# A two-layer state-space and mixture kernel: scans moved from 128 channels to 4 states x 32 channels on the partitions

## The chip, the cores and the metric

One core of a Trainium2 chip runs the whole program. The metric is the device time of one execution in microseconds (us). The engines are named as in the profile: PE multiplies matrices, DVE and POOL work elementwise (DVE also scans), ACT evaluates functions, SP issues the transfers (DMA).

## The reference

The input is `x`, 2 batches of 256 channels and 4096 positions, all in float32. It goes through a normalization over groups of channels and a state-space layer (256 inner channels), then through two layer normalizations and a forward and a backward state-space layer (512 inner channels each), then through a mixture of eight small networks. Each adds to a running `t`. The state-space layer is what matters here:

```
xs, z = split(seq @ W_in)                  # din inner channels each
xc    = silu(causal_conv4(xs))
dbc   = xc @ W_x                           # 16 for dt, 16 B, 16 C
dt    = softplus(dbc[:16] @ W_dt + b_dt)   # per channel and position
h[d,s] = h[d,s] * exp(dt[d] * A[d,s]) + dt[d] * xc[d] * B[s]     # along the 4096 positions
y[d]   = sum over s of h[d,s] * C[s] + xc[d] * D[d]
out    = (y * silu(z)) @ W_out
```

There are 16 states `s`, and `h` is carried along all positions.

## The kernel before

**Work.** Six jobs run one after the other: the first layer for two batches (2 blocks of 128 channels), the forward layer for two batches and the backward layer for two batches (4 blocks). Each job goes over its 4096 positions in 8 chunks of 512: 48 steps in `steps`, 16 narrow ones (`nj` = 2) and 32 wide ones (`nj` = 4). The mixture stage follows at the end.

**Quads.** In a step the scans go in quads `(i, jp, n)`: one pair `jp` of blocks and one pair `n` of states, so four rows of 128 partitions x 512 positions. A narrow step has 8 quads, a wide one 16. A partition is a channel. Per quad:
- SP loads two tiles, two rows of B and two of C, each spread from DRAM over all 128 partitions (`load_bc`, 512 KB each; the tile is called `bc`).
- POOL forms `bq = xdt * B` (`emit_b`, L533), where `xdt = dt * xc` is formed once per pair of blocks (L531).
- ACT forms the decays `da = exp(dt * a)` into PSUM, two per half quad (`emit_decay`, L546).
- DVE scans four rows (`emit_scan`, L556).
- The product with C is done by DVE for the quads n = 1, 4, 6, 7 (`emit_times_c`, L567) and by POOL for n = 0, 2, 3, 5 (`POOL_C`; `emit_times_c_quad`, L581). For the latter ACT first copies the last column into the carried state (`emit_carry`, L576).
- PE adds the states up into `y` in PSUM (`emit_sum`, L591) with an identity as the weight. It goes by quadrants of 64 rows x 64 columns (`TILES`). `y` starts with the skip term `xc * D` (`emit_skip`, L601), and `y` has one buffer, for a pair of blocks.
- DVE multiplies `y` with the gate `sz` (`emit_gate`, L608); PE projects (L623), DVE adds the residual (L631).

In what follows bN and cN are POOL's product with B and with C of quad N of a step (b8 in a narrow step is quad 0 of the next one).

**Order.** Every engine works strictly in the order in which the code writes to it (`in_order` ties each instruction to the one before it on its engine). The loop goes over slots, two per quad (s = 0 and 1), and in a slot writes for SP, PE, ACT, POOL and DVE in turn. Besides the scans of step i, the slots hold the preparation of step i + 1 (`prepare`): each operation is put into a slot and an engine's list by `sl.put`. In a wide step the projections and convolutions of the four blocks stand in slots 4 to 11, `dbc` in 14, and `softplus(j)` in slot 16 + j on PE, 17 + j on ACT, 18 + j on DVE; in a narrow step these are 0 to 3, 6, and 8 + j, 9 + j, 10 + j. POOL's products stand in the slots that `POOL_AT` gives:

```python
POOL_C = {0: 2, 2: 4, 3: 5, 5: 7}
POOL_AT = {0: "b3", 1: "c0 b4 b5", 3: "c2 b6", 4: "c3 b7", 6: "c5 b8 b9", 7: "b10"}
```

so at n = 1 POOL forms c of quad 0, then b of quads 4 and 5, in the first slot of that quad. `bq` has six buffers. The other tiles that matter: `dt` three buffers of a pair of blocks, `xdt` two, PSUM `ps` (projections, convolutions, dt) two.

**Buffers.** A tile whose pool has n buffers waits, when it is written the (n+1)th time, for every reader of the tile that had the buffer, a transfer among them.

## Time and profile before

| | us |
|---|---|
| median of 3 runs (6547.55 to 6551.92) | 6547.71 |
| the profiled execution | 6547.15 |
| its span, first to last instruction | 6545.3 |
| first scan | 52.1 |
| one narrow step (steps 9 to 13) | 56.4 to 56.6 |
| last narrow step, with the weights of the first wide one | 86.8 |
| one wide forward step | 119.9 |
| one wide backward step | 116.6 |

The times of the steps are from the timeline: from the first scan of a step to that of the next. A line of the profile names the source line, the engine, the operation and `out<-in` by the names of the tiles; `xN` is how many. One matrix product in float32 leaves two records. "Idle before" is how long the engine had nothing to do just before an instruction, and the arrow names what ended that. A timeline line gives the start and the length in us; neighbouring instructions of one kind are merged. A line of stretches gives, for a window of time, busy us (and the number of instructions) of PE, PE's weight loads, DVE, ACT and POOL, then the granted clock, the busy share of the DMA engines and GB/s.

### The profile page before, as it was taken

The page shows a single profiled execution, that of the slowest core. Times are in us where ns is not written, and L with a number is a line of the kernel's source. Part 1 is how long each engine was busy: PE and PEld are TensorE (multiplying, and loading weights), DVE is VectorE, ACT ScalarE, POOL GpSimd, SP SyncE. Part 2 cuts the span into 40 slices and gives each one's busy share as a digit, 9 for nine tenths or more (in the row PEclk, how much of TensorE's full clock was granted, in tenths as well). Part 3 has the DMA queues.
Part 4 walks back from the last instruction along what each step waited for, and adds up shares of the span by engine and source line. Part 5 has one row for each costly group of instructions (what it writes and reads, how often), then busy time and mean ns, then how long its engine had stood idle before and what let it go on. Part 6 is the DMA issues. An engine that isn't in the chain of part 4 may idle for free.

```text
span 6545.3 us, 53913 instructions
## 1 busy us (share of the span) xinstructions
PE 5210.1 (80%) x18600; PEld 1864.2 (28%) x18600; DVE 4695.0 (72%) x4889; ACT 3286.2 (50%) x5057; POOL 4530.5 (69%) x1062
## 2 busy tenths in 40 slices
PE   6778777877777778777777777777669999999999
PEld 2222222222222222222222222222124444444444
DVE  7999998999999999998999999999921111111111
ACT  5666665565565555655555555565522222222222
POOL 7999988999999999999999999999910000000000
PEclk9888888988988888889888898888879999999989
DMA  5545454445445444444444444444410000000000
GB/s 181 184 172 184 176 177 152 155 166 170 161 158 174 156 164 161 164 162 164 152 169 155 156 161 156 163 162 159 162 64 11 2 13 13 13 0 13 13 7 7
DMA packets 254229, 806.98 MB, mean 123 GB/s; under 512 B 26362, under 2 KB 35330, under 8 KB 253954
## 3 DMA queue, kind: packets, MB, share of 16 engines
q1 hardware_dynamic: 253954, 803.53, 35.8%
q8 instruction: 146, 2.39, 0.1%
q14 instruction: 129, 1.06, 0.1%
HBM read 749.95 MB, written 53.48 MB: 123 GB/s over the span
## 4 chain that ended last, share of the span: by engine, by line
PE 41%; DVE 34%; ACT 11%; issue 9%; POOL 4%; DMA 1%; SPq 0%; DVEq 0%; POOLq 0%; ACTq 0%
DVE da L556 16%; PE hp L863 14%; DVE bq L556 9%; PE conv L383 7%; PE ym L897 7%; ACT da L546 4%; PE y L591 4%; DVE bq L567 4%; PE xs L348 3%; POOL bq L533 2%; PE o L623 2%; POOL bq L581 1%; PE wb L888 1%; DVE xc L397 1%; DMA bc<-bcd 1%
## 5 line engine op out<-in xcount | busy, mean ns | idle before, releaser
L533 POOL TENSOR_TENSOR bq<-xdt,bc 128x2048 f32<-128x2048 f32 x640 | 2882.5, 4527 | 6.3
L546 ACT ACTIVATE da<-dt,w_a 128x512 f32<-128x512 f32 x2560 | 1766.0, 690 | 1350.9 <-DVE h_state L570 1122.5
L591 PE MATMUL y<-bq,ident 64*64 64x512 f32 x10240 | 1396.4, 666 | 477.5 <-DVE bq L567 424.7
L581 POOL TENSOR_TENSOR bq<-bq,bc 128x2048 f32<-128x2048 f32 x320 | 1448.1, 4525 | 171.0 <-ACT h_state L576 171.0
L556 DVE TENSOR_TENSOR_SCAN da<-da,h_state,bq 128x512 f32<-128x512 f32 x1120 | 1437.4, 1283 | 86.9 <-issue 66.5
L556 DVE TENSOR_TENSOR_SCAN bq<-da,h_state,bq 128x512 f32<-128x512 f32 x1120 | 1363.1, 1266 | 3.9 <-ACT da L546 2.4
L867 ACT ACTIVATE h<-hp,of,sc 128x512 f32<-128x512 f32 x512 | 397.8, 777 | 1024.8 <-PE hp L863 1024.8
L567 DVE TENSOR_TENSOR bq<-da,bc 128x1024 f32<-128x1024 f32 x640 | 783.9, 1225 | 36.9 <-DMA bc<-bcd 9.1
L894 DVE TENSOR_TENSOR h<-h,wbs 128x1024 f32<-128x1024 f32 x128 | 156.9, 1226 | 874.7 <-ACT h L867 874.7
L591 PEld LDWEIGHTS y<-bq,ident 64*64 64x64 f32 x10240 | 359.4, 146 | 1480.2 <-DVE bq L567 695.7
L383 PE MATMUL conv<-xs,w_conv 128*128 128x512 f32 x1280 | 589.4, 603 | 43.1 <-ACT xs L373 24.5
L863 PE MATMUL hp<-n,W 128*128 128x512 f32 x1024 | 490.6, 634 | 0.0
L348 PE MATMUL z<-nx,w_in 128*128 128x512 f32 x640 | 358.0, 698 | 134.1 <-DVE sz L466 109.1
L863 PE MATMUL hp<-h,W 128*128 128x512 f32 x1024 | 449.9, 592 | 0.0
L897 PE MATMUL ym<-h,Wo 128*128 128x512 f32 x1024 | 449.9, 592 | 0.0
L430 PE MATMUL dt<-dbc,w_dt 128*128 128x512 f32 x320 | 238.8, 839 | 241.4 <-DVE dt L445 191.2
L383 PEld LDWEIGHTS conv<-xs,w_conv 128*128 128x128 f32 x1280 | 233.2, 190 | 392.7 <-issue 261.5
L623 PE MATMUL o<-sz,w_out 128*128 128x512 f32 x640 | 342.7, 681 | 1.5 <-DVE sz L608 1.4
L348 PE MATMUL xs<-nx,w_in 128*128 128x512 f32 x640 | 322.8, 629 | 22.8 <-DVE xr L631 19.6
L863 PEld LDWEIGHTS hp<-n,W 128*128 128x128 f32 x1024 | 201.1, 202 | 293.3 <-issue 293.3
L890 DVE COPY wbs<-wb 128x512 f32<-128x512 f32 x64 | 44.2, 691 | 320.6 <-PE wb L888 320.6
L601 PE MATMUL y<-xc,w_d 64*64 64x512 f32 x640 | 143.4, 984 | 155.4 <-DVE sz L608 155.4
(116 smaller groups left out, 4180.4 us busy)
## 6 DMA issues: line engine op xcount, KB each, us to landing
bc<-bcd SPq DMA_DIRECT2D x1280, 512.0 KB, 4.7
t_dram<-xr SPq DMA_DIRECT2D x48, 512.0 KB, 6.1
x<-t_dram SPq DMA_DIRECT2D x32, 512.0 KB, 5.7
xr<-t_dram SPq DMA_DIRECT2D x32, 512.0 KB, 6.5
x<-in_x SPq DMA_DIRECT2D x16, 512.0 KB, 5.4
xr<-in_x SPq DMA_DIRECT2D x16, 512.0 KB, 6.3
n_dram<-nx SPq DMA_DIRECT2D x16, 512.0 KB, 2.6
t_dram<-x SPq DMA_DIRECT2D x16, 512.0 KB, 3.4
```

Source lines behind the costliest of these rows:

```text
L348: nc.tensor.matmul(ps, job.w["in"][:, k, m * P : (m + 1) * P], rhs, start=(k == 0), stop=(k == KC - 1),)
L383: nc.tensor.matmul(v["ps"], w["conv"][:, j, k, :], job.xs[:, j, k : k + T], start=(k == 0), stop=(k == 3),)
L533: nc.gpsimd.tensor_tensor(bq[g], ck["xdt", jp].rearrange("p (o j) t -> p o j t", o=1).to_broadcast([P, 2, 2, T]), bt.pop(g).rearrange("p s ...
L546: nc.scalar.activation(da[g, s][:, j, :], cks[i]["dt", jp][:, j, :], AF.Exp, scale=steps[i][0].w["a"][:, 2 * jp + j, 2 * n + s : 2 * n + s ...
L556: nc.vector.tensor_tensor_scan(b if n in POOL_C else d[:, j, :], d[:, j, :], b, job.h[:, 2 * n + s, 2 * jp + j : 2 * jp + j + 1] if c else ...
L567: nc.vector.tensor_tensor(bq[g][:, s, :, :], d, ct[g][:, s : s + 1, :].to_broadcast([P, 2, T]), ALU.mult)
L581: nc.gpsimd.tensor_tensor(bq[g], bq[g], ct[g].rearrange("p s (o t) -> p s o t", o=1).to_broadcast([P, 2, 2, T]), ALU.mult,)
L591: nc.tensor.matmul(y[i, jp][out_, r, :], ident[rows, rows], bq[g][rows, s, j, :], start=False, stop=(n == QN - 1 and s == 1),)
L623: nc.tensor.matmul(v[m], job.w["out"][:, j, m * P : (m + 1) * P], ck["sz", j // 2][:, j % 2, :], start=(j == 0), stop=(j == job.nj - 1),)
L863: nc.tensor.matmul(ps, w[:, k, m * P : (m + 1) * P], x[:, k, :], start=(k == 0), stop=(k == KC - 1),)
L867: nc.scalar.activation(h[:, m, :], ps, AF.Relu, bias=of[:, l, e, m : m + 1], scale=sc[:, l, e, m : m + 1],)
L897: nc.tensor.matmul(y[:, b, m, :], we["Wo", e][:, k, m * P : (m + 1) * P], h2[b][:, k, :], start=False, stop=(e == E - 1 and k == KC - 1),)
```

## The change

A partition now holds one of 4 states and one of 32 channels. A quad is one block `j` and one group `sg` of 4 states; its four rows `q` are the four groups of 32 channels of the block. B and C tiles hold a group of 4 states, each state copied to 32 partitions (`load_states`, 256 KB), and serve all blocks of a step: 8 loads per step, 5 buffers each. In exchange `dt` and `xdt` must be spread, so that each of four groups of 32 partitions holds all 128 channels of a block as 4 rows of 32: after DVE's `dt` and POOL's `xdt` (now one per block, written in slot s + 2 of `softplus`), SP stores both to DRAM (slots s + 3 and s + 4), and `load_rep` reads each back in four transfers of 256 KB to 32 partitions. `load_later` gives each load the slot from which it may be issued, and `flush` issues those that are due and whose source has been written. The sum over the states becomes, per quad, four products of 128 rows x 32 columns with the weight `stack`, one for each row `q`, all after the quad's end. `y` holds one block and has two buffers; skip and gate go by block. `dt` and `xdt` have two buffers of one block each. W_out is loaded when its job starts, and the skip weights later. The host reorders the decay weights, and no longer reorders z and W_out.

```diff
-QN = NS // 2
-TILES = [(r, col, (col - r) % 2) for r, col in ((0, 0), (1, 1), (0, 1), (1, 0))]
+QN = 8
+SG = 4
+CG = P // SG
+POOL_AT_2 = {**POOL_AT, 6: "c5 b8", 7: "b9 b10"}
...
-        ps_y = st.enter_context(tc.tile_pool(name="ps_y", bufs=1, space=PSUM))
+        ps_y = st.enter_context(tc.tile_pool(name="ps_y", bufs=2, space=PSUM))
...
+        stack = const.tile([P, CG], F32, name="stack")
+        nc.vector.tensor_reduce(
+            stack, ident.rearrange("p (s c) -> p c s", s=SG), AX.X, ALU.add
+        )
...
                 def dve():
-                    dt = pair_tile(ck, "dt", j, tag, 3)
-                    nc.vector.scalar_tensor_tensor(dt, v["ps"], 0.0, v["th"], ALU.max, ALU.add)
-                    if j % 2:
-                        ck["dt_done", j // 2] = True
-                return pe, act, dve
+                    v["dt"] = wk.tile([P, T], F32, tag="dt", name=f"dt_{tag}_{j}", bufs=2)
+                    nc.vector.scalar_tensor_tensor(v["dt"], v["ps"], 0.0, v["th"], ALU.max, ALU.add)
+
+                def pool():
+                    v["xdt"] = wk.tile([P, T], F32, tag="xdt", name=f"xdt_{tag}_{j}", bufs=2)
+                    nc.gpsimd.tensor_tensor(v["xdt"], v["dt"], ck["xc", j], ALU.mult)
+
+                def store(key):
+                    d = ck["rep", key, j] = bcd.tile(
+                        [P, T], F32, tag=f"{key}{j}", name=f"{key}d_{tag}_{j}"
+                    )
+                    nc.sync.dma_start(d, v[key])
+
+                return pe, act, dve, pool, lambda: store("dt"), lambda: store("xdt")
...
             def put(s, fns):
-                for d, queue, fn in zip(range(3), ("pe", "act", "dve"), fns):
+                queues = ((0, "pe"), (1, "act"), (2, "dve"), (2, "pool"), (3, "sp"), (4, "sp"))
+                for (d, queue), fn in zip(queues, fns):
...
+        def load_states(i, h, sg):
+            t = bcp.tile([P, T], F32, tag=f"bc{h}", name=f"bc{h}_{tags[i]}_{sg}", bufs=5)
+            src = cks[i]["bc"][h, sg * SG : (sg + 1) * SG, :]
+            nc.sync.dma_start(
+                t, src.rearrange("s (o t) -> s o t", o=1).to_broadcast([SG, CG, T])
+            )
+            cks[i]["bc", h, sg] = t
+
+        def load_rep(i, key, j):
+            t = wk.tile([P, SG, T], F32, tag=f"r{key}", name=f"r{key}_{tags[i]}_{j}", bufs=2)
+            src = cks[i]["rep", key, j].rearrange("(q c) t -> c q t", q=SG)
+            for s in range(SG):
+                nc.sync.dma_start(t[s * CG : (s + 1) * CG], src)
+            cks[i]["r" + key, j] = t
+
+        def load_later(i, slot):
+            nj = steps[i][0].nj
+            for sg, (b, c) in enumerate(((-16, -16), (-13, -6), (-12, -1), (-9, 0))):
+                pending.append((slot + b, ("bc",), lambda sg=sg: load_states(i, 0, sg), i))
+                pending.append((slot + c, ("bc",), lambda sg=sg: load_states(i, 1, sg), i))
+            for j in range(nj):
+                for key, off in (("xdt", (-10, -12)[j % 2]), ("dt", -4)):
+                    pending.append(
+                        (slot + 8 * j + off, ("rep", key, j), lambda j=j, key=key: load_rep(i, key, j), i)
+                    )
+            pending.sort(key=lambda p: p[0])
+
+        def flush(slot):
+            for p in list(pending):
+                if p[0] <= slot and (p[1] if len(p[1]) > 1 else p[1][0]) in cks[p[3]]:
+                    pending.remove(p)
+                    p[2]()
...
+            nc.gpsimd.tensor_tensor(bq[g], ck["rxdt", j], over_groups(ck["bc", 0, sg]), ALU.mult)
...
+                    da[g, h][:, k, :], cks[i]["rdt", j][:, q, :], AF.Exp,
+                    scale=steps[i][0].w["a"][:, j, q * SG + sg : q * SG + sg + 1],
...
+        def emit_sum(g):
+            i, j, sg = at(g)
+            for q in range(SG):
+                nc.tensor.matmul(
+                    y[i, j][q * CG : (q + 1) * CG, :], stack, bq[g][:, q, :],
+                    start=False, stop=(sg == SG - 1),
                 )
...
-                    if first == 2 and last is not None:
-                        emit_gate(*last)
-                        last = None
-                    if first == 3:
-                        emit_skip(i, jp)
+                    if first in (2, 12) and done:
+                        emit_gate(*done.pop(0))
+                    if first in (1, 9):
+                        emit_skip(i, 2 * jp + first // 8)
...
-                    if s == 0:
-                        for what in POOL_AT.get(n, "").split():
+                    if h == 0:
+                        for what in (POOL_AT if wide else POOL_AT_2).get(n, "").split():
                             m = g - n + int(what[1:])
                             if what[0] == "c":
                                 emit_times_c_quad(m)
                             else:
-                                want(0, m + 3)
-                                flush()
                                 want_b(m)
-                    else:
-                        want(1, g + 2)
-                        flush()
                     sl.run(slot, "pool")
```

## The prediction

> **What bounds the kernel now.** I read the page first (engine shares), then the stretches of one step of each kind, then the timelines of POOL, DVE and PE inside them, then the waits.
>
> The page's first part gives busy time by engine, and its DMA issues give the median time to landing:
>
> ```profile
> PE 5210.1 (80%) x18600; PEld 1864.2 (28%) x18600; DVE 4695.0 (72%) x4889; ACT 3286.2 (50%) x5057; POOL 4530.5 (69%) x1062
> ...
> bc<-bcd SPq DMA_DIRECT2D x1280, 512.0 KB, 4.7
> n_dram<-nx SPq DMA_DIRECT2D x16, 512.0 KB, 2.6
> gx<-in_x SPq DMA_DIRECT2D x4, 1024.0 KB, 8.2
> ```
>
> The last quarter is the mixture stage, which the diff leaves alone. In the scans the stretches of one narrow step, one wide forward step and one wide backward step (start to start of the first scan) show who is full:
>
> ```profile
> core 0: us, PE busy (x) PEld busy (x) DVE busy (x) ACT busy (x) POOL busy (x), PEclk, DMA share, GB/s
> 579.30:635.90 56.60, 44.05 (x185) 13.48 (x184) 54.98 (x59) 36.74 (x57) 56.52 (x14) 0.91 0.54 179
> 2448.20:2568.20 120.00, 90.51 (x376) 28.61 (x376) 112.05 (x116) 70.55 (x112) 114.60 (x28) 0.88 0.48 163
> 3971.80:4088.40 116.60, 85.82 (x368) 27.65 (x368) 108.96 (x115) 66.24 (x105) 112.89 (x27) 0.88 0.46 160
> ```
>
> A narrow step is POOL from end to end (56.5 of 56.6). A wide step has 5.4 us (forward) or 3.7 us (backward) without POOL and some 8 us without DVE. DMA is half used, and the bytes that the change saves are on no path. What DVE waits for in the wide steps is seen in its waits between 2000 and 4000 us (17 steps):
>
> ```profile
> DVE xc L397 <- ACT thx L393: 73.8, 51, 2.0
> DVE da L556 <- issue: 36.3, 17, 2.4
> ```
>
> Both come from PE. Its timeline of one wide step (start, length, then the instructions merged):
>
> ```profile
> 2454.13 1.99 PE L601 MATMUL y<-xc,w_d 64*64 64x512 f32 x8 [3.91 <-DVE sz L608]
> ...
> 2472.65 3.60 PE L383 MATMUL conv<-xs,w_conv 128*128 128x512 f32 x8
> ...
> 2482.20 1.95 PE L591 MATMUL y<-bq,ident 64*64 64x512 f32 x16
> ```
>
> PE waits for the one `y` buffer until 2454.1, then works to 2502 with 0.6 us of gaps; the convolution, its tanh and `xc` come late in that stretch. Eight full records take 3.60 us (0.45 each), sixteen quadrant records 1.95 us (0.12): four quadrants run at once.
>
> **The change, part by part.** *Nothing on DVE, ACT or POOL gets shorter.* Four scans (1.28 us), one product with C (1.22 us per half) and one product with B (4.53 us) per quad keep shape and count. Gates go from 80 of 1.20 to 160 of about 0.68 us: 0.1 us per wide step. `xdt` goes from one 2.36 us product per pair to two of 128x512; from 4.53 for 2048 and 2.36 for 1024 elements I estimate 1.27, so 0.2 us more per pair on POOL.
>
> *Sums (PE).* Per quad 16 records in four quadrants (1.9 us) become 8 records in four 32-column strips. Bounds: 0.9 us if four strips run at once, 8 x 0.45 = 3.6 us if they run singly. I take 0.9: the L591 row already shows two column strips fed different data over the same rows. The second `y` buffer takes the 2 us skip out of the stretch after 2454. By the wide step's second block PE has then saved 1.9 us of skip and four halved groups of 0.47, 3.8 us, so the 2.1 us before the scan at 2474.8 and the 1.6 us before `xc` at 2477.8 go; I count 3.3, as tanh and add behind the convolution stay. The other two `xc` waits (0.8, 1.8 us) lie in a part that becomes POOL's, below.
> The page "TensorE: Matmul & The Clock Gate", Part 3, of the Trainium skill gives 2.38x for three 32-column tiles; at that efficiency the sum would be an estimated 1.14 us per quad, 0.6 us of relief would be missing per wide step, and the total would be 18 us higher. No row here shows 32-column tiles.
>
> *dt buffers (DVE), wide steps.* `dt` is now two buffers, freed by POOL's `xdt` and by the store. `xdt` for block j stands in POOL's order behind slot 18 + j, so behind c8, b12, b13 of quad 9 (on the trace of before: the products that end at 2530.7).
>
> ```profile
> 2492.35 4.53 POOL L581 TENSOR_TENSOR bq<-bq,bc 128x2048 f32<-128x2048 f32 x1 [3.88 <-ACT h_state L576]
> 2496.84 2.36 POOL L531 TENSOR_TENSOR xdt<-dt,xc 128x1024 f32<-128x1024 f32 x1
> 2499.28 17.94 POOL L533 TENSOR_TENSOR bq<-xdt,bc 128x2048 f32<-128x2048 f32 x4
> 2517.17 4.53 POOL L581 TENSOR_TENSOR bq<-bq,bc 128x2048 f32<-128x2048 f32 x1
> 2521.65 9.03 POOL L533 TENSOR_TENSOR bq<-xdt,bc 128x2048 f32<-128x2048 f32 x2
> ```
>
> DVE did its third dt at 2525.42. Now POOL first runs those eight products (8 x 4.48 = 35.84) and `xdt` of block 0 (1.3): DVE gets its third dt 37.15 us after c5 starts, and stalls some 5 us with the scans behind it. From there to the end of quad 5's scans in the next step took DVE 84.7 us forward (2525.4 to 2490.3 + 119.9) and 81.4 backward (4048.8 to 4013.7 + 116.6); less 3.3, plus 0.4 for the carry copy, plus 0.4 or 0.3 for the `dt` and `xdt` of blocks 2 and 3, which wait for stores that SP issues behind that of block 0. Forward 37.15 + 84.7 - 3.3 + 0.8 = 119.3 against 119.9; backward 37.15 + 81.4 - 3.3 + 0.7 = 115.9 against 116.6. So the wait eats the relief: 15 x 0.6 + 15 x 0.7 = 20 us gained. Ends: no relief, +4.0 and +3.9 a step, +119; all of it until POOL alone paces, -51: forward 37.15, 6.3 to the start of c10 (two dt, three scans, the centring and the carry lie between), and 74.2 of products and the add, 117.7; backward 37.15 + 5.2 + 71.7 and 1.4 of waiting before c13, 115.4.
>
> *Spreading xdt (POOL), narrow steps.* POOL's order there:
>
> ```profile
> 616.26 4.56 POOL L533 TENSOR_TENSOR bq<-xdt,bc 128x2048 f32<-128x2048 f32 x1
> 620.75 4.54 POOL L581 TENSOR_TENSOR bq<-bq,bc 128x2048 f32<-128x2048 f32 x1
> 625.24 2.36 POOL L531 TENSOR_TENSOR xdt<-dt,xc 128x1024 f32<-128x1024 f32 x1
> 627.68 13.48 POOL L533 TENSOR_TENSOR bq<-xdt,bc 128x2048 f32<-128x2048 f32 x3
> ```
>
> Now it is b7, xdt0, xdt1, c5, b8, and b8 needs xdt0 stored and loaded again (1 MB in four issues). The cover is xdt1 and c5: 5.8 us. The store: between 1.8 us (the SP timeline has the 64 KB `bcd` store at 607.53 and the load that waits for it at 609.30) and 2.6; I take 2.1. The load: between 4.7 (512 KB) and 8.2 (1 MB, queued with others); I take 4.7 + 1.5, as 803.5 MB in 35.8% of 6545 us is 343 GB/s. That is 8.3, a wait of 2.5, with 0.2 for `xdt` 2.7 us per step (0.9 to 5.2). POOL has nothing to hide it. The first four steps take 58.7 us and hide 2.3 of it: 11 x 2.7 + 4 x 0.4 = 31 us lost (10 to 70). Behind b8 on POOL stand b9 to b11; DVE has 3.7 us of lead on b8, used up after two steps.
>
> *Start and the narrow-to-wide boundary.* Before the first scan (52.1) xdt and dt must be stored and loaded: 2 MB until xdt0, 1.5 MB more until dt0, from 46.8 on; with 4.7 us for the first 512 KB and 1.5 for each further that is 56.0 and 60.5, first scan near 61: +9 (5 to 18). At step 16 the loads of `xdt` stand on SP behind the stores of normalized x, which wait for POOL's add at 1000.5: its first b starts near 1007, against 1002.9: +4 (0 to 12). W_out, the skip weights and the decay order move off any path.
> The page "DMA: Bandwidth & Descriptors", section on why a semaphore rises by 16, says that a transfer uses only as many engines as divide the outermost size of both sides: four for the new B and C loads (four states). By that the four ahead of xdt0 at the start take an estimated 6 us more, and the total is 6 us higher. No row shows it.
>
> *Sum:* 9 + 31 - 20 + 4 = +24 us on the profiled execution (6547.15 with its 6545.3 span, 0.6 below the median): 6572 against 6547.7.
>
> **Rivals.** *Faster:* PE's relief reaches DVE whole, so POOL alone paces the wide steps: -51, narrow +10, ends +5: about 6512. For it: PE is full in the very stretch before each wait. Against: the third dt stands behind POOL whatever PE does. It decides once a wide step gains over 1.5 us (44 us over 30).
> *No relief:* the strips run at most two at a time, or another wait takes PE's place: +119 + 31 + 13, 6711. For: no row of 32-column tiles.
> *Strips one by one:* 1.7 us more PE per quad, 640 x 1.7 = 1088 us, of which PE's idle quarter hides perhaps 600: about 7000. Against: L591's quadrants.
>
> **How the numbers follow.** Forecast 0.46 (6540 to 6605), faster 0.26 (6495 to 6550), no relief 0.18 (6650 to 6760), strips singly 0.10. The range 6502 to 6715 leaves out the last and the tails. A difference under 0.2% (13 us) cannot be told from none: faster 0.22, same 0.20 (0.16 of the forecast, 0.04 of the first rival), slower 0.58.
>
> **What would show it.** Right: L591's mean busy time per quad near 0.9 us; DVE waiting for POOL's `xdt` at the third dt, about 5 us in each wide step; POOL waiting for a DMA before the first b of each narrow step, 1 to 5 us; narrow steps near 59 us, wide near 119 and 116; `xc` waits mostly gone. Wrong: 32-column sums over 1.9 us per quad; scans or products of another length; a load of dt late for the decays; wide steps under 117.

## The result, and the profile after

The changed kernel takes 7049.1 us (median of 4 runs, 7046.65 to 7055.2) against 6548.6 for the kernel before: ratio 1.0765 [1.0746, 1.0783], 501 us slower. The prediction said 6572 (6502 to 6715): the sign was right, the loss twenty times too small, and the time lies far outside the range. The profiled execution took 7055.2 us with a span of 7053.4.

The page of the changed kernel: busy time by engine, the DMA queue (packets, MB, share of 16 engines), and the group of the sums.

```profile
PE 5102.3 (72%) x13160; PEld 1794.3 (25%) x13160; DVE 4703.5 (67%) x4970; ACT 3292.8 (47%) x5057; POOL 4538.5 (64%) x1142
...
q1 hardware_dynamic: 350722, 652.56, 37.0%
...
L631 PE MATMUL y<-bq,stack 128*32 128x512 f32 x5120 | 1009.2, 762 | 676.5 <-DVE bq L613 340.4
```

DVE, ACT and POOL have the same work as before to within 9 us; the 501 us are waiting. The queue moves 652.6 MB where it moved 803.5, and yet holds the engines for a larger share of a longer span. The stretches of the same three steps as before (narrow step 9, wide forward 28, wide backward 41):

```profile
core 0: us, PE busy (x) PEld busy (x) DVE busy (x) ACT busy (x) POOL busy (x), PEclk, DMA share, GB/s
652.70:715.00 62.30, 41.92 (x116) 12.63 (x116) 55.13 (x59) 36.86 (x58) 56.49 (x15) 0.86 0.59 145
2695.10:2823.80 128.70, 84.82 (x240) 26.72 (x240) 112.39 (x119) 70.95 (x112) 114.88 (x30) 0.79 0.47 119
4394.40:4526.60 132.20, 87.87 (x232) 26.56 (x232) 109.38 (x117) 66.37 (x105) 113.59 (x30) 0.77 0.44 109
```

In none of them is an engine full: POOL has 5.8 us free in the narrow step that it filled before, and 14 to 19 us in the wide ones. By the starts of the steps' first scans (the last row to the end of the last scan):

| us | before | after | difference | predicted |
|---|---|---|---|---|
| first scan | 52.1 | 81.4 | +29.3 | +9 |
| narrow steps 0 to 14 | 869.7 | 955.9 | +86.2 | +31 |
| step 15, to the first wide scan | 86.8 | 107.2 | +20.4 | +4 |
| steps 16 to 31, nearly all forward | 1917.3 | 2070.7 | +153.4 | -9 |
| steps 32 to 47, backward | 1849.2 | 2068.5 | +219.3 | -11 |

What DVE waits for between 2000 and 4000 us (the releaser behind the arrow; us in total, times, longest), and POOL in the whole run:

```profile
DVE dt L455 <- POOL xdt L459: 98.8, 16, 6.4
DVE sz L644 <- PE y L631: 82.9, 31, 5.7
...
DVE xc L407 <- ACT thx L403: 24.5, 15, 1.7
```

```profile
POOL xdt L459 <- DMA xdtd<-xdt: 283.2, 55, 17.4
...
POOL bq L585 <- DMA rxdt<-xdtd: 124.1, 14, 21.7
```

Before, xc (73.8 us) headed DVE's list. Now the wait at the third dt is there (6 us a step, some 5 predicted), the gate (`sz<-y`) is new, and POOL waits above all for the *store* of an earlier xdt to free its buffer. In the forward step these places on POOL's timeline are:

```profile
2763.78 4.53 POOL L626 TENSOR_TENSOR bq<-bq,bc 128x2048 f32<-128x2048 f32 x1 [2.24 <-ACT h_state L622]
2768.26 8.97 POOL L585 TENSOR_TENSOR bq<-rxdt,bc 128x2048 f32<-128x2048 f32 x2
2777.20 2.48 POOL L459 TENSOR_TENSOR xdt<-dt,xc 128x512 f32<-128x512 f32 x2
2780.66 1.26 POOL L459 TENSOR_TENSOR xdt<-dt,xc 128x512 f32<-128x512 f32 x1 [0.98 <-DMA xdtd<-xdt]
2790.07 1.26 POOL L459 TENSOR_TENSOR xdt<-dt,xc 128x512 f32<-128x512 f32 x1 [8.15 <-DMA xdtd<-xdt]
```

c8 waits 2.24 us for ACT's copy of the carried state, the two xdt behind it release DVE's third dt at 2778.5, and the fourth xdt waits 8.15 us; in the backward step 41 it waits 12.4:

```profile
4493.84 1.27 POOL L459 TENSOR_TENSOR xdt<-dt,xc 128x512 f32<-128x512 f32 x1 [12.38 <-DMA xdtd<-xdt]
```

The copy that c8 waits for comes late by ACT's order, not by DVE's scans: these end at 2761.2, and the copy then stands behind the softplus of the first block. The copy ahead of c5 stands in the same way behind a tanh that waits for PE's convolution:

```profile
2756.40 4.80 DVE L604 TENSOR_TENSOR_SCAN bq<-da,h_state,bq 128x512 f32<-128x512 f32 x4
...
2762.90 0.72 ACT L451 ACTIVATE sp<-sp,one_col 128x512 f32<-128x512 f32 x1
2763.53 0.18 ACT L622 COPY h_state<-bq 128x4 f32<-128x4 f32 x1
```

```profile
2737.49 0.69 ACT L402 ACTIVATE thx<-conv,w_cb 128x512 f32<-128x512 f32 x1 [1.15 <-PE conv L393]
2738.21 0.72 ACT L403 ACTIVATE thx<-thx,one_col 128x512 f32<-128x512 f32 x1
2738.84 0.18 ACT L622 COPY h_state<-bq 128x4 f32<-128x4 f32 x1
```

In backward steps the late fourth xdt reaches DVE through the gate: POOL's products with C behind it come later, PE's last sum of the block with them, and the gate waits for that sum. Between 3215 and 5177 us (the backward steps) this is DVE's largest wait, some 7.2 us a step:

```profile
DVE sz L644 <- PE y L631: 108.9, 30, 7.3
```

Why the store is late shows in SP's issues, first in the narrow step:

```profile
697.14 0.34 SPq L465 DMA_DIRECT2D xdtd<-xdt  x1
697.58 0.38 SPq L465 DMA_DIRECT2D dtd<-dt  x1
701.59 1.76 SPq L547 DMA_DIRECT2D rxdt<-xdtd  x4
703.44 1.80 SPq L547 DMA_DIRECT2D rdt<-dtd  x4
705.34 0.38 SPq L465 DMA_DIRECT2D xdtd<-xdt  x1
```

POOL finished the second xdt at 698.3, but its store is issued at 705.3: SP first waited until the first store had landed (701.6), then issued eight loads. POOL's first b got its operand only at 708.6 (5.81 us idle). In the wide step the larger part comes after the issue:

```profile
2778.48 0.34 SPq L465 DMA_DIRECT2D xdtd<-xdt  x1
2778.92 0.38 SPq L465 DMA_DIRECT2D dtd<-dt  x1
2779.35 1.93 SPq L547 DMA_DIRECT2D rdt<-dtd  x4
2781.32 0.53 SPq L537 DMA_DIRECT2D bc<-bcd  x1
2781.95 0.42 SPq L465 DMA_DIRECT2D xdtd<-xdt  x1
```

POOL finished the second xdt at 2779.7; its store is issued 2.3 us later, behind five loads, and POOL's fourth xdt, which needs the store landed, starts only at 2790.1, 8.1 us after the issue (11.9 in the backward step 41). The semaphores in the trace show what the store waits for: twelve of its sixteen parts land 4.7 to 5.1 us after the issue, behind the four loads of dt, and the last four at 2789.4 to 2789.9, just behind the four parts in which the B or C load issued ahead of it lands (2789.0 to 2789.5). In e1 below, with no load ahead, all sixteen parts of the second store land 2.0 to 2.2 us after the issue.

### The profile page after: what moved, and what is told of

Its sections match the earlier page's. It is cut to its first block, busy times and chain, and to the rows that moved or that the text cites. A ratio compares the mean times of both kernels' runs of the same rounds, so it can differ in the third digit from the quotient of the medians.

```text
span 7053.4 us, 43766 instructions
## 1 busy us (share of the span) xinstructions
PE 5102.3 (72%) x13160; PEld 1794.3 (25%) x13160; DVE 4703.5 (67%) x4970; ACT 3292.8 (47%) x5057; POOL 4538.5 (64%) x1142
## 4 chain that ended last, share of the span: by engine, by line
PE 32%; POOL 19%; DVE 15%; issue 9%; DMA 6%; ACT 2%; SPq 1%; POOLq 0%; DVEq 0%; ACTq 0%
POOL bq L585 14%; PE hp L893 13%; DVE da L604 8%; PE ym L927 6%; POOL bq L626 5%; DMA xdtd<-xdt 4%; PE conv L393 3%; DVE bq L604 3%; PE y L631 3%; PE xs L363 3%; DVE bq L613 2%; DMA rdt<-dtd 1%; POOL xdt L459 1%; PE wb L918 1%; DMA rxdt<-xdtd 1%
## 5 line engine op out<-in xcount | busy, mean ns | idle before, releaser
L585 POOL TENSOR_TENSOR bq<-rxdt,bc 128x2048 f32<-128x2048 f32 x640 | 2880.6, 4525 | 146.7 <-DMA rxdt<-xdtd 124.1
L594 ACT ACTIVATE da<-rdt,w_a 128x512 f32<-128x512 f32 x2560 | 1766.5, 690 | 1844.8 <-DVE h_state L617 1117.9
L631 PE MATMUL y<-bq,stack 128*32 128x512 f32 x5120 | 1009.2, 762 | 676.5 <-DVE bq L613 340.4
L363 PE MATMUL z<-nx,w_in 128*128 128x512 f32 x640 | 419.5, 802 | 198.8 <-DVE sz L484 101.6
L631 PEld LDWEIGHTS y<-bq,stack 128*32 128x32 f32 x5120 | 161.5, 124 | 1474.1 <-DVE bq L613 571.2
L363 PE MATMUL xs<-nx,w_in 128*128 128x512 f32 x640 | 374.2, 715 | 215.3 <-DVE xr L667 192.0
L440 PE MATMUL dt<-dbc,w_dt 128*128 128x512 f32 x320 | 271.4, 945 | 322.9 <-DVE dt L455 179.3
L459 POOL TENSOR_TENSOR xdt<-dt,xc 128x512 f32<-128x512 f32 x160 | 200.7, 1268 | 403.2 <-DMA xdtd<-xdt 283.2
L659 PE MATMUL o<-sz,w_out 128*128 128x512 f32 x640 | 307.8, 632 | 17.2 <-DVE sz L644 14.8
L363 PEld LDWEIGHTS z<-nx,w_in 128*128 128x128 f32 x640 | 152.3, 255 | 485.0 <-DVE sz L484 163.8
```

The costliest lines, as they stand in the source:

```text
L363: nc.tensor.matmul(ps, job.w["in"][:, k, m * P : (m + 1) * P], rhs, start=(k == 0), stop=(k == KC - 1),)
L585: nc.gpsimd.tensor_tensor(bq[g], ck["rxdt", j], over_groups(ck["bc", 0, sg]), ALU.mult)
L594: nc.scalar.activation(da[g, h][:, k, :], cks[i]["rdt", j][:, q, :], AF.Exp, scale=steps[i][0].w["a"][:, j, q * SG + sg : q * SG + sg + 1],)
L631: nc.tensor.matmul(y[i, j][q * CG : (q + 1) * CG, :], stack, bq[g][:, q, :], start=False, stop=(sg == SG - 1),)
L659: nc.tensor.matmul(v[m], job.w["out"][:, j, m * P : (m + 1) * P], ck["sz", j], start=(j == 0), stop=(j == job.nj - 1),)
```

## The experiments

**One edit at a time on the changed kernel.** "SP order" moves the wide steps' B, C, dt and xdt loads to slots in which no load stands between the four blocks' stores:

```diff
-            for sg, (b, c) in enumerate(((-16, -16), (-13, -6), (-12, -1), (-9, 0))):
+            for sg, (b, c) in enumerate(
+                ((-16, -16), (-7, -6), (-6, -1), (-5, 0)) if nj == 4 else
+                ((-16, -16), (-13, -6), (-12, -1), (-9, 0))
+            ):
...
-                for key, off in (("xdt", (-10, -12)[j % 2]), ("dt", -4)):
+                for key, off in (("xdt", (-8, -12)[j % 2]), ("dt", -7)) if nj == 4 else (("xdt", (-10, -12)[j % 2]), ("dt", -4)):
```

> In the wide steps the loads of B and C tiles 1 to 3 and of dt are issued a few slots earlier or later, so that SP has no load between the stores of dt and xdt (slots 19 to 23); nothing else changes. Theory 'queue': POOL's fourth xdt waits 8 to 12 us because the store that frees its buffer lies behind five loads. Then that wait falls to about 2 us, a wide forward step from 129 to about 121, a backward one from 131 to about 120, DVE's wait at the third dt (6 us) stays, narrow steps stay at 63; about 6750 us in all. Theory 'slow transfers' (each transfer is slow by its form, whatever its place): the wide steps move by under 2 us, about 7000 us.

Measured 6914.4, ratio 1.0559 [1.0528, 1.0589], -135. The fourth xdt's wait falls to 0.3 us forward and 2.7 backward:

```profile
2764.56 1.27 POOL L459 TENSOR_TENSOR xdt<-dt,xc 128x512 f32<-128x512 f32 x1 [0.29 <-DVE dt L455]
```

Backward steps go from 131.0 to 124.0 (means of steps 33 to 39 and 41 to 46), forward ones (17 to 23 and 25 to 29) only from 129.4 to 128.0. Summed over DVE's timeline, its waits fall by 6.8 us in a backward step (20.7 to 13.9, of it 5.0 at the gate), and by 1.2 in a forward one (16.2 to 15.0). So the late store paces the backward steps; forward, 8 us of POOL's wait were worth 1.4, since little of it reaches DVE.

The form of the B and C loads: four loads of one state to 32 partitions in place of one load of four states.

```diff
-            nc.sync.dma_start(t, src.rearrange("s (o t) -> s o t", o=1).to_broadcast([SG, CG, T]))
+            for s in range(SG):
+                nc.sync.dma_start(t[s*CG:(s+1)*CG], src[s:s+1, :].rearrange("s t -> (s t)").partition_broadcast(CG))
```

> Each load of a B or C tile (4 states, 256 KB) becomes four loads of one state to 32 partitions (64 KB each), so that the outermost size is 32 on both sides. Theory 'four engines': the 2 to 3 us by which each such load holds back what is behind it go to under 1 us; narrow steps, with five of them ahead of the stores, from 63 to about 58, wide steps by 2 to 3 us; about 6890 us. Theory 'queue' without it: narrow steps unchanged or slower by the 24 more transfers of a step, wide steps unchanged; about 7050 us.

Measured 6933.7, ratio 1.0588 [1.0558, 1.0619], -115: first scan at 70.9, narrow steps (9 to 13) 63.3 to 59.9, step 15 107.2 to 99.4, wide steps 1.3 (forward) and 2.2 (backward) shorter. The bytes are the same; the form and the number of transfers differ.

The round trip's latency: loads of dt and xdt read one old copy in DRAM, so they need not wait for the store just made.

```diff
-            src = cks[i]["rep", key, j].rearrange("(q c) t -> c q t", q=SG)
+            src = stale[key].rearrange("(q c) t -> c q t", q=SG)
```

> The spread loads read one copy of dt and xdt stored before the first step, instead of the block's own (so the values of dt and xdt from the first block stand in for all others); stores, loads, their number and order stay. Theory 'round trip' (store, then load, before the first b and decay of a step): narrow steps lose their waits before b8 and the decays, from 63 to about 58; wide steps do not change (their loads have slots to spare); about 6970 us. Theory 'queue': the same in the wide steps, and the narrow ones stay within 2 us of 63, because dt and xdt are late by what lies ahead of them.

Measured 7036.0, ratio 1.0744 [1.0713, 1.0776], -13: narrow steps 61.7, forward ones unchanged, backward ones 0.8 shorter. That SP waits for the store before it loads is worth under 2 us a narrow step; the form of the B and C loads ahead of it is worth more (e2).

Channel-major partitions, (channel, state) in place of (state, channel), so that each load writes 128 partitions:

```diff
-                t, src.rearrange("s (o t) -> s o t", o=1).to_broadcast([SG, CG, T])
+                t, src.rearrange("(o s) t -> o s t", o=1).to_broadcast([CG, SG, T])
...
-            for s in range(SG):
-                nc.sync.dma_start(t[s * CG : (s + 1) * CG], src)
+            for q in range(SG):
+                nc.sync.dma_start(t[:, q, :], src[q].to_broadcast([CG, SG, T]))
```

> The partitions hold 32 channels x 4 states with the state innermost, instead of 4 states x 32 channels; each spread load then goes to all 128 partitions (256 KB, one row group per load) and each B or C load has 32 as its outermost size on both sides; numbers of transfers, bytes and order stay. Theory 'four engines' and 'slow transfers': loads follow one another at 0.7 instead of 1.1 us and B, C loads at under 1 us instead of 3; the fourth xdt's wait falls from 8 to 12 us to about 4, narrow steps to about 58, wide to 124; about 6800 us. Theory 'queue' alone: under 2 us per step.

Measured 6863.2, ratio 1.0481 [1.045, 1.0511], -186, the largest single gain: first scan at 61.5, narrow 59.2, step 15 98.0, backward 126.3, forward 128.0. Its queue line, beside the changed kernel's 37.0% for the same bytes, shows 26% less engine time (28.3% of 6862.8 against 37.0% of 7053.4):

```profile
q1 hardware_dynamic: 355330, 652.58, 28.3%
```

What the two forms cost can be read from stretches of the changed kernel in which almost only one kind of transfer runs (columns as above; the last two are the busy share of the 16 DMA engines and GB/s): B and C loads, stores from 128 partitions, and loads of dt and xdt to 32 partitions.

```profile
684.00:688.00 4.00, 4.00 (x8) 1.18 (x4) 4.00 (x5) 3.39 (x6) 4.00 (x2) 0.50 0.26 101
689.00:690.50 1.50, 0.18 (x4) 0.00 (x0) 0.70 (x2) 1.47 (x3) 1.50 (x1) 1.00 1.04 404
705.00:711.00 6.00, 4.21 (x14) 0.97 (x12) 5.18 (x7) 0.00 (x0) 2.38 (x1) 0.97 1.07 212
```

B and C loads keep a quarter of the engines busy and move 101 GB/s, so one of 256 KB takes an estimated 2.6 us; four of them in a row landed 2.6 us apart. The dt and xdt loads keep all of them busy at half the rate of the stores. Per busy engine the B and C loads are as quick as the stores, so the 26% of e4 come from the dt and xdt loads; e2, which changes B and C alone, leaves the engine time as it was (37.5% of 6935).

Three edits of order: xdt earlier on POOL, the gate of the odd block later on DVE, the residual adds earlier on DVE.

```diff
+POOL_AT_4 = {**POOL_AT, 1: "c0 b4", 2: "b5"}        # e5, wide steps
-                    if first in (2, 12) and done:
+                    if first in (2, 14) and done:    # e6
-                sl.put(s0 + m + 2, "dve", lambda m=m: add(m))
+                sl.put(s0 + m + 1, "dve", lambda m=m: add(m))   # e7
```

> In the wide steps POOL takes xdt one product earlier in its order (the second of b4, b5 moves from behind it to the next slot). Theory 1 (the third dt on DVE waits for POOL's xdt and paces the forward wide steps): the wait of 6.1 us at the third dt falls to about 2, the forward wide steps from 128.9 to about 125; the backward ones stay near 130.5, because there POOL is paced by the store ahead of its fourth xdt. Total about 6990. Rival (this wait only takes the place of one that PE or the gate would cause): the forward steps stay within 1 us of 128.9 and another DVE wait grows by what this one loses; total 7049.

Measured 7068.1, ratio 1.0794 [1.0773, 1.0816], 19 us *slower*. The third dt's wait falls from 6.13 to 1.67 us, but the fourth dt now waits 4.14 for the store that frees its buffer (5.81 together), and the second gate waits 2.61 where it waited 1.07. The rival holds here; the wait moved.

> The gate of the odd block of each pair is emitted two tiles of scans later (first == 14 in place of 12), so that PE's last sum of that block has ended when DVE comes to it. Theory 1 (the wait of 2.1 us of the gate for PE's y is a wait on DVE's path): it goes in both blocks of a wide step, forward steps 128.9 to about 126, total about 7000. Rival (DVE only arrives earlier at the wait for xdt): the third dt's wait grows by the same amount and the total stays near 7049.

Measured 6962.1, ratio 1.0632 [1.0611, 1.0653], -87. The gate's wait is gone. The moved gate stands twice in a wide step, and the two waited 3.7 us forward and 7.2 backward (2.13 and 5.73 in step 41). Forward steps gain 1.2 us (new waits of 0.5 and 0.95 at xc), backward ones 4.7; the total is 38 us lower than expected, since I had counted 2.1 for each.

> DVE's residual adds stand one slot earlier in its order, so that the two PSUM buffers of the output projection come free earlier for the next step's in_proj and convolution. Theory 1 (these two buffers, not PE's throughput, set the waits of 1.6 to 2.3 us around xc and quad 4's first scan): the waits shrink by 3 to 6 us in all per wide step; forward steps 128.9 to about 124 to 126, total about 6980. Rival (PE's throughput sets them): the waits stay, total 7049. Third possibility: the adds themselves now wait for PE's output projection and the time only moves: total near 7049 with a new wait at the add.

Measured 6960.0, ratio 1.0629 [1.0608, 1.065], -89: forward 126.8, backward 128.6. The waits up to the first xc (1.75, 1.22, 1.63 in step 28 of the changed kernel, 5.0 on average of steps 17 to 46) fall to 2.6 on average; in step 28 alone only one of 0.80 is left. They came from PE standing still, not from PE being full:

```profile
2712.41 3.61 PE L363 MATMUL xs<-nx,w_in 128*128 128x512 f32 x4 [6.65 <-DVE xr L667]
2715.95 1.92 PE L631 MATMUL y<-bq,stack 128*32 128x512 f32 x16
2717.81 1.98 PE L363 MATMUL xs<-nx,w_in 128*128 128x512 f32 x4
...
2725.55 3.70 PE L393 MATMUL conv<-xs,w_conv 128*128 128x512 f32 x8 [0.60 <-DVE xc L407]
```

In this timeline of the changed kernel PE idles 6.65 us until DVE's residual add frees one of the two PSUM buffers, and only then projects for the next step. The pause costs a second time: the projection after it takes 3.61 us, the same four records next time 1.98. The clock that the throttle granted PE is 0.50 of full speed from 2708.9 to 2715.7 and 1.00 behind that. In e7 29 of the 30 steps 17 to 46 still begin with a projection of 2.6 to 3.8 us at a clock of 0.50 to 0.73, after a pause of 3.1 us or more; step 28, after 2.88, has 1.95 us at a clock of 1.00, and it is the step with the one wait of 0.80.

**All edits together, then each left out.** e8 has SP order, channel-major partitions, the three order edits, and in narrow steps b7 moved behind the two xdt, so that POOL has a product to do during the round trip.

> The channel-major partitions, the stores ahead of the loads on SP, xdt one product earlier, the gate later, the adds earlier, and in narrow steps b7 behind the two xdt so that POOL has work during the round trip. If the waits that were named are the whole loss: narrow steps near 57, wide ones near 118 forward and 116 backward, start 61, total 6500 to 6600, within 1% of the kernel before. If they overlap, so that each removed wait shows another: wide steps 122 to 126, total 6700 to 6800. A total below 6500 would show that the 32-column sums bring a gain once the copies are out of the way.

Measured 6560.8, ratio 1.0018 [1.0008, 1.0027]: 488 of the 501 us are back. Narrow steps take 56.6, as in the kernel before (56.5). POOL goes without a gap from the xdt into the products of the next block:

```profile
625.44 2.51 POOL L460 TENSOR_TENSOR xdt<-dt,xc 128x512 f32<-128x512 f32 x2
627.90 4.54 POOL L589 TENSOR_TENSOR bq<-rxdt,bc 128x2048 f32<-128x2048 f32 x1
632.37 4.53 POOL L630 TENSOR_TENSOR bq<-bq,bc 128x2048 f32<-128x2048 f32 x1
636.85 13.49 POOL L589 TENSOR_TENSOR bq<-rxdt,bc 128x2048 f32<-128x2048 f32 x3
```

> The version with all edits (6561), but with the load offsets of the changed kernel in the wide steps, so that loads stand on SP between the stores again. Theory 1 (the wait of POOL's fourth xdt for its store is a cost of its own): backward wide steps go from 116.3 to 121 to 126, forward from about 121 to 122 to 126; total 6650 to 6800; narrow steps stay at 56.6. Rival (the layout over 128 partitions makes the loads so fast that their order no longer matters): within 0.5% of 6561.

> The version with all edits, but with state-major partitions as in the changed kernel: B and C loads over four engines, copies of dt and xdt into 32 partitions at a time. Theory 1 (the slow form of the loads costs by itself): start near 80 in place of 62, narrow steps 59 to 62 in place of 56.6, boundary step 100 to 105 in place of 91, wide steps within 3 us of 121 and 116; total 6650 to 6750. Rival (once POOL has work during the round trip the form of the loads is hidden): total within 0.5% of 6561, apart from 18 us of start.

> The version with all edits, but with the gate and the residual adds on DVE at their places in the changed kernel. Theory 1 (the chain DVE add, PSUM buffer, in_proj, convolution, and the gate's wait for the last sum, pace the forward wide steps by themselves): forward steps 121 to 124 to 126, backward within 1 us of 116.3; total 6610 to 6660. Rival (these waits only filled time in which POOL was late): within 0.3% of 6561.

> The version with all edits, but with POOL's order of the changed kernel. The narrow order shows in the narrow steps, the wide order in the wide ones, so one run tells both. Theory 1 (narrow: the round trip of xdt is hidden only by moved products): narrow steps from 56.6 to 58.5 to 59.5, +22 to +32 over 11 to 15 steps; wide: the third dt waits 6.1 again in place of 1.7, forward steps 121 to 124 to 125.5, backward +0 to +2; total 6620 to 6680. Rival (the faster loads of the new layout hide the trip without help, and the wide order is worth nothing, as the earlier xdt alone did not help): within 0.3% of 6561.

| kernel | us | against e8 | same edit alone on the changed kernel | narrow | forward | backward |
|---|---|---|---|---|---|---|
| e8, all | 6560.8 | | | 56.6 | 121.1 | 116.5 |
| e9, without SP order | 6577.6 | +17 | -135 | 56.6 | 121.2 | 117.4 |
| e10, without channel-major | 6658.3 | +97 | -186 | 60.8 | 121.0 | 116.5 |
| e11, without gate and adds | 6645.2 | +84 | -87 and -89 | 56.2 | 123.3 | 119.3 |
| e12, without POOL order | 6730.7 | +170 | +19 (wide part) | 59.1 | 125.6 | 120.8 |

(Ratios to the kernel before: 1.0045 [1.0029, 1.0061], 1.0165 [1.0145, 1.0185], 1.0147 [1.0127, 1.0167], 1.0276 [1.0256, 1.0297].) For e9 the rival holds: once loads are quick, their order hardly matters. e10 came out as theory 1 had it, but for step 15 (106.4 where I had 100 to 105); e11 in its total, but forward steps took 123.3 where I had 124 to 126, and backward ones lost 2.8 us where I had said under 1. e12 costs more than either theory allowed: some 29 us are the narrow steps' product (870.6 to 900.1 for steps 0 to 14), the rest is 4.4 us in every wide step, with the third dt at 6.13 us again. So the wide edit that lost 19 us alone is the dearest to leave out. Waits in a ring of engines cover one another; the price of an edit depends on which others are in.

**Is PE's relief worth anything?** Each sum made twice on a halved stack of ones gives PE its work back:

```diff
+        nc.vector.tensor_scalar(stack, stack, 0.5, None, ALU.mult)
...
+                for r in range(2):
                     nc.tensor.matmul(..., start=False, stop=(sg == SG - 1 and r == 1))
```

> The version with all edits, with each 32-column sum made twice on a halved stack of ones (half plus half is exact): PE's sums take 1.8 to 2.0 us per quad again, as with the 64-column sums of the kernel before, 640 x 0.9 = 580 us more work on PE. Theory 1 (the waits around xc and quad 4 come through the two PSUM buffers and DVE's adds, and PE's relief is worth nothing): total within 0.5% of 6561. Rival (the relief is worth the 3.3 us per wide step that the prediction counted): +90 to +106, about 6660.

> The changed kernel itself, with each sum made twice on a halved stack of ones. The prediction's words were that the wait for xdt eats PE's relief. If so, PE's work can be given back at little cost: total within 0.7% of 7049, with the wait at the third dt or at the fourth xdt smaller by what the xc waits grow. Rival (the relief is worth as much here as beside all edits): +100 to +130, about 7165.

e13 takes 6679.6, ratio 1.0203 [1.0188, 1.0218], +119 on e8. e18 takes 7194.6, ratio 1.0984 [1.0968, 1.1], +146 on the changed kernel. In both my theory fell, and the cost is even above the rival's range (+90 to +106 and +100 to +130): PE's work is on the path, 3.5 to 3.9 us per wide step in e13 and 4 to 5 in the changed kernel. In e18 the third dt waits 6.13 us as ever, and other waits grow beside it: the one before quad 4's scan from some 1.5 to 3.3 us in a forward step, and the gate's (82.9 us in the same stretch of the changed kernel):

```profile
DVE sz L646 <- PE y L633: 117.1, 29, 6.7
DVE dt L456 <- POOL xdt L460: 92.8, 15, 6.4
```

Doubling is more than the change saved: the sums' group goes from 1024.1 us in e8 to 1629.8 in e13, where the kernel before had 1396.4; so these prices are for more work than the change had taken off PE. The doubling also raises the granted clock (0.855 in e8, 0.905 in e13; 0.824 in the changed kernel, 0.875 in e18), so they are not the price of PE's work at one clock.

**Whose gain are the order edits?** e14 is the kernel before with its adds one slot earlier. e15 is e8 with the output projection and adds of wide steps one slot earlier still and xdt one product earlier still; e16 is e14 with the same move of projection and adds; e17 is e15 with each sum twice.

```diff
-                finish(i - 1, 3 if wide else 5, sl)
+                finish(i - 1, 2 if wide else 5, sl)              # e15, e16
-POOL_AT_4 = {**POOL_AT, 1: "c0 b4", 2: "b5"}
+POOL_AT_4 = {**POOL_AT, 1: "c0", 2: "b4 b5"}                     # e15
```

> The kernel before with its residual adds one slot earlier on DVE, and nothing else. Theory 1 (the same two PSUM buffers pace the kernel before): its 2.1 us before quad 4 and 1.6 us before xc shrink by 1 to 3.5 us per forward step; total 6500 to 6535. Rival (there PE's throughput sets these waits, or another takes their place): total within 0.2% of 6548.

> The version with all edits, with the output projection and the adds of the wide steps one slot earlier still, and xdt one product earlier still. Theory 1: of the forward step's waits 0.7 to 2.0 before quad 4's scan, 1.63 at xc and 1.68 at the third dt go: 121 to 117 to 118.5, backward 116.3 within 1 us (POOL paces it); total 6490 to 6530, faster than both kernels. Rival (new waits take their place, as when xdt alone was moved): 6550 to 6600.

> The kernel before with its residual adds one slot earlier and its output projection and adds one further slot earlier in the wide steps, as in e15. If these order edits are what made e15 faster, this kernel gains as much: 6430 to 6470. If e15's lead is the sums' relief of PE (3.7 us per wide step by e13), this one stays behind it: 6500 to 6530, forward steps 118.5 to 119.5.

> e15 with each sum made twice on a halved stack of ones. If the relief of PE is what lies behind e15's lead: 6550 to 6590 (+100 to +140). If the earlier adds made PE's time free: within 0.5% of 6450.

| kernel | us | ratio to before | narrow | forward | backward |
|---|---|---|---|---|---|
| e14 | 6523.5 | 0.9963 [0.9948, 0.9977] | 56.5 | 119.4 | 116.1 |
| e15 | 6450.5 | 0.9848 [0.9834, 0.9863] | 56.6 | 117.1 | 112.9 |
| e16 | 6443.8 | 0.9836 [0.982, 0.9853] | 56.5 | 116.5 | 113.6 |
| e17 | 6523.6 | 0.9959 [0.9944, 0.9974] | 56.7 | 119.4 | 115.9 |

e15 and e16 beat the kernel before by 1.5 and 1.6%, and their intervals overlap: with its order mended, the kernel before is as fast as the changed scheme with its order mended. The waits of e15 on DVE between 2000 and 4000 us have neither the third dt nor the gate any more:

```profile
DVE xc L408 <- ACT thx L404: 44.1, 53, 1.6
DVE dt L456 <- ACT sp L452: 12.7, 18, 0.9
DVE cen L317 <- PE mean L311: 5.3, 6, 1.0
```

e14's time came out as theory 1 had it, but not its place: the wait before quad 4 fell only from 2.10 to 1.78 us and that at xc stayed at 1.63. e16 fell into its first range; e15 went below its own (6490 to 6530), as backward steps gained 3.5 us where I had said under 1. e17 lies between its two cases: of e15's lead over the kernel before, 73 of 98 us go when PE's sums are made twice.

## Why the prediction was wrong, point by point

- **Unchanged work: right.** DVE's and POOL's busy times moved by under 9 us; xdt measured 1.26 us (1.27 estimated), the gate 0.67 (0.68). Four such gates in place of two of 1.20 are 0.3 us per wide step, not the 0.1 that I wrote.
- **Sums: right in kind, too good in size.** Four 32-column strips run at once: at a granted clock of 1.00 eight records of one quad take 1.07 us, sixteen 1.92, where eight full ones take 3.70, so the rival "strips one by one" is out, though its 7000 us was nearest to the time. The page "TensorE: Matmul & The Clock Gate", Part 3, of the Trainium skill gives 2.38x for three such tiles; here four give 3.70 / 1.07 = 3.5x. By group the mean is 1.58 us per quad (1009.2 / 640) against 2.18 before (1396.4 / 640): 0.6 saved, where I counted 1.0. I priced every sum at the speed of the full clock. In steps 17 to 46 eight records took 1.07 us where the granted clock was 1.00 and 1.94 where it was 0.50 (64 groups each), and the clock averaged 0.79 over forward step 28 (0.88 before).
- **"So the wait eats the relief": this step failed.** Wide steps were to gain 20 us and lost 373. I had POOL go from c5 to the third dt in one block of 37.15 us; it took 39.39 (2739.10 to 2778.49), and the 2.24 more is c8 waiting for the carry copy, which stands behind softplus on ACT: with xdt gone from between them POOL came to c8 earlier, but c8 starts 24.7 us after c5 where it had been 24.8. From the third dt to c5 of the next step (2868.24) it took 89.7 where I had 82.2: 3.3 of relief that did not come, 1.3 of longer waits ahead of xc (5.0 against 3.7), 1.07 at the gate, 0.84 at the centring, and 1.5 at the carry copy: I had 0.4 for it, but it stands behind the tanh that waits for PE, and c5 starts 1.86 us after quad 5's scans (2866.38 to 2868.24). The 0.4 for blocks 2 and 3 was not needed. The third dt waits 6.1 us, as said, but DVE and POOL wait for each other by turns, so that a wait on one is not paid by a wait on the other; I let them hide behind one another. e18 shows it: slower sums lengthen the step while the third dt's wait stays. The end "no relief" does not follow from the same sum either: without the 3.3 it gives +2.7 a step, not +4.0.
- **The relief of 3.3 us ahead of xc did not come.** PE was full in that stretch of the kernel before (0.6 us of gaps), and I took it that less work there brings the convolution forward. In the changed kernel PE waits there for DVE's adds through two PSUM buffers, 6.65 us in step 28, and then projects at half the clock; e7 shows that moving the adds shortens the waits. What the half clock costs by itself no run shows. DVE's waits in forward step 28 come to 15.5 us (1.75, 1.22, 1.63, 2.14, 0.68, 6.13, 0.84, 1.07) against 6.8 before, with DVE's busy time the same 112 us: that is the 8.7 us of the step. The gate at `first == 12`, which the change adds in the middle of a pair, I had at its duration, with no wait.
- **Stores behind loads: mis-sized most in backward steps.** I gave dt and xdt of blocks 2 and 3 0.3 to 0.4 us, which wait for SP's order; POOL's fourth xdt waits 8 and 12 us, most of it after the store is issued. e1 takes 7.0 us out of a backward step; with the quick loads of e8 the same order is worth 1.0 (e9).
- **Narrow steps: the right wait, 2.7 us predicted, 6.8 measured** (63.3 against 56.5). Of this the form of the B and C loads is 3.4 (e2), the wait for the store 1.6 (e3), and with all edits nothing is left (e8). The cover I priced (xdt1 and c5) was right, the length of the trip was not: from 697.1 to 708.6 it is 11.5 us for 8.3, the store 4.4 (2.1 taken) and the loads 7.0 (6.2). The store shares the engines with B and C loads of 2.6 us each.
- **Start and boundary: +9 and +4 predicted, +29.3 and +20.4 measured.** With channel-major loads the start is +9.4 and step 15 +11.2 (e4). The step that failed is the price of the loads' form. The page "DMA: Bandwidth & Descriptors" of the Trainium skill says that a transfer runs on the largest number of engines, at most 16, that divides the outermost size of both sides. For the B and C loads that is four, and the trace agrees: a DMA share of 0.26 while they run, and landings in four parts. I took an estimated 6 us for it at the start alone; e2, which changes that form, gains 115. The rule spoke against the change, and I let it touch one place where it touched every step. For the loads to 32 partitions I had one price from loads to 128; e4, which changes both forms, gains 186.
- **Rivals.** "No relief: another wait takes PE's place" named the right kind of outcome; its 6711 had no late store, no slow loads and no wait at the gate in it. "Faster" needs the order edits of e15, and then the kernel before gains as much.

What stays open: no run moves the carry copies on ACT or holds the clock, so what either is worth by itself is not shown, nor is any edit's price beside each subset of the others.

## What to carry to other kernels

When two in-order engines hand tiles to each other several times per step, waits on either can add up: lay the hand-overs out as one chain over both and do not let one engine's wait pay for another's. Before taking an engine as full, see what ends its idle time; here it was PSUM buffers that a cheap add on another engine held, and a copy of four columns that stood behind longer work on a third. For every transfer that a change adds, price its form (how many partitions or engines the outermost dimension gives it) at every place of the step, and look at which stores stand behind it on the same queue, since these free the buffers.

## What the runs showed of the hardware

- 256 KB loads whose outermost size is four (4 states, each to 32 partitions) ran at 101 GB/s with a DMA share of 0.26; 256 KB loads to 32 partitions, four rows in each, at 212 GB/s with all engines busy; stores from 128 partitions at 404 GB/s. With every load spread over 128 partitions the same 652.6 MB hold the engines 26% less long (e4).
- Four 32-column strips of float32 products with different data run nearly fully at once, the last strip included: 16 records in 1.92 us, where eight full records take 3.70.
- The granted TensorE clock in these traces is 0.50 or 1.00, and 0.50 was seen behind pauses of PE: four records of a projection took 3.61 us at 0.53 and 1.98 at 1.00, eight records of the sums 1.94 at 0.50 and 1.07 at 1.00. The mean over a run went roughly with PE's busy share: 0.824 at 72% (changed kernel), 0.859 at 77% (e15), 0.900 at 80% (e16), 0.914 at 83% (e17). The convolutions, which run in the full-clock part of a step, took 3.6 to 3.7 us in nearly all steps before and after, so the mean clock of a step does not give the time of its products.
